# A graph layer's message loop in a written order, with PSUM banks shared by four groups and fewer, larger loads

## The chip, the cores and the metric

The kernel runs on one core of one Trainium2 chip. The core has five engines that run their own instruction queues: TensorE (PE; its weight loads are shown apart as PEld), VectorE (DVE), ScalarE (ACT), GpSimd (POOL) and SyncE (SP, which only issues transfers here). Results of TensorE go to PSUM, eight banks of 2 KB in each of 128 partitions; all else lives in SBUF or in device memory. The metric is device microseconds of one execution, the median of several.

## The reference

One layer of a graph network over 12,500 nodes (96 features) and 412,500 edges (4 features), the edges sorted by their target node. Cut to what matters:

```python
def mlp(h, W, b, gamma, beta):            # batch norm over all rows
    h = relu(h @ W + b)
    mu, var = mean(h, axis=0), mean(square(h - mean(h, axis=0)), axis=0)
    return gamma * (h - mu) * rsqrt(var + EPS) + beta

node_feat = mlp(x, W_node, b_node, g_node, beta_node)
edge_feat = mlp(edge_attr, W_edge, b_edge, g_edge, beta_edge)
message = concatenate([x[src], x[dst], edge_feat], axis=1)       # 412500 x 288
message = mlp(message, W_msg, b_msg, g_msg, beta_msg)
agg = segment_sum(message, dst, 12500)
out = layernorm(x + agg + node_feat)
```

## The kernel before, in words

All arithmetic is fp32. `x[src] @ W` and `x[dst] @ W` are not computed per edge: two tables in device memory, `p_tab` and `q_tab`, hold `x` times the two parts of `W_msg`. An edge's row of `p_tab` is fetched by an indirect transfer on GpSimd (L289), one instruction for 128 edges. `q_tab` needs no gather, since edges are sorted: 512 consecutive edges (a *group*, four tiles of 128) reach at most WN = 30 consecutive nodes, a window of `q_tab` that one matmul spreads over the edges.

There are 806 groups, and BG = 4 groups make a *block* (202 of them). The stages are:

1. **First table** (`table`, L136, called at L154): `p_tab`, in 7 chunks of 14 matmuls; PSUM tiles `pt` hold 4, 4, 4 and 2 of them, and DVE and ACT copy them out in turn. Then window offsets (`rel`, and `rel_d` in device memory, L191 to L200), by SP's loads `lin` and `first`.
2. **Second table** (`table` again, L310): `q_tab`, with four PSUM tiles `pt`. GpSimd already gathers the rows of the first 104 groups, 26 blocks (`blocks`, L297). Two staging buffers take a block each, 16 gathers, and SP writes each to device memory (`spill`, L303). The order of SP and GpSimd is written by hand here: the first spill stands behind the fourth chunk of `q_tab`, three more behind the seventh.
3. **Nodes** (L202): node features and their norm.
4. **Edge statistics** (`edge_norm`, L234): a first pass over the edge features. For each block of 2,048 edges, three matmuls of 512 columns into one PSUM tile of three banks (two such tiles), one ACT relu over the 1,536 columns (L252), three BN_STATS on DVE (L254). Features come in chunks of eight blocks (L245). Of 26 chunks, 19 have a spill behind them on SP.
5. **The message loop** (L326 to L430), over blocks in an order that mixes the 26 early blocks among the 176 late ones. For a late group GpSimd gathers into a ring of 30 buffers (`ring`, `ahead_of`, L294), 30 groups ahead. An early block's rows come back by one load (`fetch`, L401).
6. **End**: the final norm and layer norm (L598 to L631).

In the loop, per block: `load` (L342) fetches the block's edge features `ea`, one row of window offsets `rel_d`, and four windows of `q_tab` into `rhs`. `prepare` (L356) makes, by four matmuls into `pr` (four PSUM banks), the relu of the edge features (ACT, L364) and the 0/1 rows that select a node of the window (DVE, L365), both into `left`. Per group: `message` (L367) makes `z` by four matmuls of `left` with `rhs` (L371), writes the 0/1 columns of the target nodes into `h` (DVE, L373), adds the gathered rows (DVE, `hs`, L377; this frees the ring's buffer) and applies the relu (ACT, L378). `reduce` (L380) multiplies `h` with itself (L386, four matmuls accumulating into `pa`), which gives both the sums per node and the Gram matrix that the batch norm needs, and adds them to `agg` (L389) and `gram` (L390) on DVE. It runs one group behind `message`.

Edge features come from an array `eaq` in which each of the four groups of a block takes 32 partitions, of which 5 are used (4 features and a one) and the rest are zeros. In the loop a scheduler puts the instructions of each engine in order by itself; only the stages before it have a hand-written order, and that for SP and GpSimd alone. PSUM in the loop: four banks for `pr`, two for `z`, two for `pa`.

Of the kernel before, what the change touches and what calls it, by code (L numbers as in the profile page):

```python
# [50 lines left out]
WN = 30  # L51
# [3 lines left out]
RING = 30  # L55
J = 8
# [14 lines left out]
def gnn(ctx, tc, t):  # L71
# [64 lines left out]
    def table(out, w, work, ps, queues):  # L136

        rows = out.rearrange("(p b) f -> p b f", b=NB)
        for c in range(0, NB, CH):
            r = work.tile([P, CH, C], F32, name="trow", bufs=3)  # L140
            for j, i in enumerate(range(0, CH, NBK)):
                n = min(NBK, CH - i)
                pt = ps.tile([P, NBK, C], F32, name="pt", bufs=4)
                for g in range(n):
                    k = COL[c + i + g]
                    nc.tensor.matmul(pt[:, g, :], xp[:, k:k + P], w, start=True, stop=True)  # L146
                if j % 2:
                    nc.scalar.activation(r[:, i:i + n, :], pt[:, :n, :], AF.Copy)  # L148
                else:
                    nc.vector.tensor_copy(r[:, i:i + n, :], pt[:, :n, :])  # L150
            queues[c // CH % len(queues)].dma_start(rows[:, c:c + CH, :], r)
            yield

    with tc.tile_pool(name="win_w", bufs=1) as work, tc.tile_pool(name="win_ps", bufs=2, space=PSUM) as ps:  # L154
        for _ in table(p_tab, w_msg[:, 0, :], work, ps, (nc.sync, nc.scalar)):
            pass
# [77 lines left out]
    def edge_norm():  # L234

        with tc.tile_pool(name="es", bufs=2) as work, tc.tile_pool(name="es1", bufs=1) as one, \
                tc.tile_pool(name="es_ps", bufs=2, space=PSUM) as ps:
            stats = one.tile([P, NS, NBL, 6], F32, name="estats")
            for b in range(NBL):
# [7 lines left out]
                pr = ps.tile([P, NS, GE], F32, name="pr")  # L247
                for i in range(NS):
                    nc.tensor.matmul(pr[:, i, :], wide[Q * i:Q * i + 2 * EK, :],  # L249
                                     ea[Q * i:Q * i + 2 * EK, b % J, :], start=True, stop=True)  # L250
                r = work.tile([P, NS, GE], F32, name="r")
                nc.scalar.activation(r, pr, AF.Relu)  # L252
                for i in range(NS):
                    nc.vector.bn_stats(stats[:, i, b, :], r[:, i, :])  # L254
# [30 lines left out]
    def fast(ring):  # L285
# [22 lines left out]
        with tc.manual_schedule(engines={ET.SP, ET.Pool}):  # L308
            with tc.tile_pool(name="tab_w", bufs=1) as work, tc.tile_pool(name="tab_ps", bufs=2, space=PSUM) as ps:
                for i, _ in enumerate(table(q_tab, w_msg[:, 1, :], work, ps, (nc.sync,))):  # L310
                    if i in (3, 6):
                        next(store)
# [12 lines left out]

        with tc.tile_pool(name="fix", bufs=1) as fix, tc.tile_pool(name="msg", bufs=2) as work, \  # L326
# [3 lines left out]
            rhs = fix.tile([P, 2, BG, C], F32, name="rhs")  # L330
            nc.vector.tensor_copy(rhs[:C], w_e[:, None, None, :].to_broadcast([C, 2, BG, C]))
            for i in range(2):
                for k in range(BG):
                    nc.sync.dma_start(rhs[KR - 1:KR, i, k, :], bias)
# [3 lines left out]
            hb = [fix.tile([P, GT, P], F32, name=f"h{i}") for i in range(4)]  # L338
# [3 lines left out]
            def load(s, b):  # L342

                n = min(BG, NG - b * BG)
                ea = work.tile([P, GE], F32, name="ea")
                nc.sync.dma_start(ea, t["eaq"][:, b, :])
                nc.sync.dma_start(ea[EK:P:Q, :], rel_d[:, b * BG * GE:(b + 1) * BG * GE]
                                  .rearrange("o (g e) -> (o g) e", g=BG))
                _, val = nc.values_load_multi_w_load_instructions(
                    base[:, b * BG:(b + 1) * BG], engines=[ET.DVE, ET.SP], min_val=0, max_val=N - 1,  # L350
                    skip_runtime_bounds_check_because="they are nodes' numbers")
                for i in range(n):
                    nc.sync.dma_start(rhs[C:C + WN, s % 2, i, :], q_tab[bass.ds(val[i], WN), :])
                return ea, val

            def prepare(s, b, ea):  # L356

                n = min(BG, NG - b * BG)
                x = left[s % 2]
                pr = ps.tile([C + WN, BG, GE], F32, name="pr", bufs=1)  # L360
                for i in range(n):
                    nc.tensor.matmul(pr[:, i, :], we[Q * i:Q * i + EK + 1, :],  # L362
                                     ea[Q * i:Q * i + EK + 1, :], start=True, stop=True)
                nc.scalar.activation(x[:C, :n, :], pr[:C, :n, :], AF.Relu)  # L364
                nc.vector.tensor_scalar(x[C:C + WN, :n, :], pr[C:, :n, :], 0.0, None, op0=OP.is_equal)  # L365

            def message(s, g, h, pg):  # L367
                n = min(GT, NT - g * GT)
                z = ps.tile([P, GT, C], F32, name="z")
                for i in range(n):  # L370
                    nc.tensor.matmul(z[:, i, :], left[s % 2][:KR, g % BG, i * P:(i + 1) * P],  # L371
                                     rhs[:KR, s % 2, g % BG, :], start=True, stop=True)
# [7 lines left out]
            def reduce(g, h, val):  # L380

                n = min(GT, NT - g * GT)
                pa = ps.tile([C + 1, P], F32, name="pa")
# [4 lines left out]
                to = agg[:, bass.ds(val, WN)]  # L388
# [4 lines left out]
            early, late = list(range(SPILL // BG)), list(range(SPILL // BG, NBL))  # L393
            order = []
            for i, b in enumerate(late):
                order.append(b)
                while early and (SPILL // BG - len(early)) * len(late) < i * (SPILL // BG):
                    order.append(early.pop(0))
            order += early

            def fetch(b):  # L401
                if b * BG < SPILL:
                    back = work.tile([P, BG, GT, C], F32, name="pb")
                    nc.sync.dma_start(back, spill[b].rearrange("p g (a c) -> p g a c", a=GT))
                    for i in range(BG):
                        got[b * BG + i] = back[:, i, :, :]

            ea, val = load(0, order[0])
            prepare(0, order[0], ea)
            fetch(order[0])  # L410
            last, n, ahead = None, 0, SPILL + RING
            for s, b in enumerate(order):
                more = s + 1 < len(order)
                if more:
                    ea, then = load(s + 1, order[s + 1])
                    fetch(order[s + 1])
                for g in range(b * BG, min((b + 1) * BG, NG)):
                    if g % BG == 1 and more:
                        prepare(s + 1, order[s + 1], ea)
                    h = hb[n % len(hb)]  # L420
                    n += 1
                    message(s, g, h, got.pop(g))
                    if last:
                        reduce(*last)
                    last = g, h, val[g % BG]
                    if g >= SPILL and ahead < NG:
                        got[ahead] = ahead_of(ahead)
                        ahead += 1
                val = then
            reduce(*last)  # L430
# [237 lines left out]
```

## Time and profile before

| | us |
|---|---|
| time, median of 3 (4302.92 to 4304.81) | 4303.69 |
| the profiled execution's own time | 5713.74 |
| its span | 5712.0 |
| POOL busy, idle before its gathers | 3070.7, 1884.8 + 608.1 |
| PE busy | 3507.9 |
| DVE busy | 1830.5 |
| ACT busy | 1126.2 |

The profiled execution took 1410.05 us longer than the median, so its parts can't be read as parts of the median without asking which of them the recording lengthens. A busy time is that of instructions alone; transfers issued by an engine aren't counted as its work, save the indirect ones of GpSimd[...]. In the lists, "L289 POOL DMA_INDIRECT pg<-p_tab,src" is line, engine, operation, and what it writes from what; "issue" is waiting for which the profile shows no cause, and "remote" is a releaser that it can't name. In the timelines the columns are start, duration, then the instruction, and in brackets the engine's idle time before it with its releaser.

The core moved 315.48 MB in 190,423 packets. The largest issues, by the page:

```profile
ea<-in_eaq SPq DMA_DIRECT2D x202, 256.0 KB
pg<-p_tab,src POOLq DMA_INDIRECT x2807
spill<-stage SPq DMA_DIRECT2D x26, 768.0 KB
pb<-spill SPq DMA_DIRECT2D x26, 768.0 KB
rhs<-q_tab SPq DMA_DIRECT2D x806, 11.2 KB
```

### The profile page before, as it was taken

The page shows a single profiled execution, that of the slowest core. Times are in us where ns is not written, and L with a number is a line of the kernel's source. Part 1 is how long each engine was busy: PE and PEld are TensorE (multiplying, and loading weights), DVE is VectorE, ACT ScalarE, POOL GpSimd, SP SyncE. Part 2 cuts the span into 40 slices and gives each one's busy share as a digit, 9 for nine tenths or more (in the row PEclk, how much of TensorE's full clock was granted, in tenths as well). Part 3 has the DMA queues.
Part 4 walks back from the last instruction along what each step waited for, and adds up shares of the span by engine and source line. Part 5 has one row for each costly group of instructions (what it writes and reads, how often), then busy time and mean ns, then how long its engine had stood idle before and what let it go on. Part 6 is the DMA issues. An engine that isn't in the chain of part 4 may idle for free. (4 is left out here: it accounts for less than half of the span.)

```text
span 5712.0 us, 52958 instructions
## 1 busy us (share of the span) xinstructions
PE 3507.9 (61%) x16561; PEld 2613.4 (46%) x16561; DVE 1830.5 (32%) x4227; ACT 1126.2 (20%) x1304; POOL 3070.7 (54%) x3231
## 2 busy tenths in 40 slices
PE   3445666146666666766667566676566666665768
PEld 3331111024545455555555455455455555554547
DVE  1134555142323223232222232232322222322326
ACT  0113444021111111111111111111111111111113
POOL 2254444725555565555565555655555655556550
PEclk9955555557776666566666766666666666666667
DMA  3232323212222222222222222222222222222212
GB/s 117 73 97 56 70 63 68 47 42 51 52 52 49 46 50 52 50 52 49 52 46 51 50 51 49 47 52 49 51 50 52 46 50 52 49 52 46 50 44 82
DMA packets 190423, 315.48 MB, mean 55 GB/s; under 512 B 95817, under 2 KB 96201, under 8 KB 189128
## 3 DMA queue, kind: packets, MB, share of 16 engines
q0 software_dynamic: 103136, 158.62, 13.2%
q1 hardware_dynamic: 83502, 141.01, 8.9%
q10 hardware_dynamic: 3496, 12.36, 0.7%
q8 instruction: 137, 2.24, 0.2%
q14 instruction: 152, 1.25, 0.1%
HBM read 270.34 MB, written 41.37 MB: 55 GB/s over the span
## 5 line engine op out<-in xcount | busy, mean ns | idle before, releaser
L289 POOL DMA_INDIRECT pg<-p_tab,src x2807 | 2670.2, 951 | 1884.8 <-issue 787.5
L371 PE MATMUL z<-rhs,left 127*128 127x96 f32 x6446 | 1330.3, 350 | 706.3 <-issue 385.0
L371 PEld LDWEIGHTS z<-rhs,left 127*128 127x128 f32 x6446 | 1181.7, 261 | 1158.2 <-issue 684.0
L386 PE MATMUL pa<-h 128*97 128x127 f32 x6446 | 1236.4, 355 | 656.2 <-issue 351.7
L386 PEld LDWEIGHTS pa<-h 128*97 128x97 f32 x6446 | 1077.7, 230 | 719.8 <-issue 377.2
L378 ACT ACTIVATE h<-hs 128x384 f32<-128x384 f32 x806 | 419.5, 521 | 3094.3 <-DVE hs L377 1528.7
L389 DVE TENSOR_TENSOR agg<-pa,agg 97x30 f32 x806 | 150.4, 187 | 1978.1 <-PE z L371 752.6
L377 DVE TENSOR_TENSOR hs<-z,pg 128x384 f32<-128x384 f32 x702 | 390.2, 556 | 1054.7 <-issue 471.4
L289 POOL DMA_INDIRECT stage<-p_tab,src x416 | 399.6, 961 | 608.1 <-DMA spill<-stage 428.3
L362 PE MATMUL pr<-ea,we 6*126 6x512 f32 x1612 | 601.4, 841 | 157.4 <-issue 102.5
L249 PE MATMUL pr<-ea,wide 10*128 10x512 f32 x1212 | 406.6, 1107 | 409.2 <-ACT r L252 264.8
L254 DVE BATCH_NORM_STATS2 estats<-r 128x6 f32<-128x512 f32 x606 | 372.1, 680 | 442.6 <-ACT r L252 287.2
L364 ACT ACTIVATE left<-pr 96x2048 f32<-96x2048 f32 x202 | 376.3, 1863 | 549.9 <-remote 260.7
L365 DVE TENSOR_SCALAR left<-pr 30x2048 f32<-30x2048 f32 x202 | 462.9, 2292 | 43.8 <-ACT left L364 37.6
L249 PEld LDWEIGHTS pr<-ea,wide 10*128 10x128 f32 x1212 | 114.5, 307 | 700.0 <-ACT r L252 484.4
L252 ACT ACTIVATE r<-pr 128x1536 f32<-128x1536 f32 x202 | 292.2, 1451 | 592.9 <-remote 384.4
L362 PEld LDWEIGHTS pr<-ea,we 6*126 6x126 f32 x1612 | 150.6, 232 | 226.0 <-issue 150.3
L373 DVE TENSOR_TENSOR h<-rel,iota 128x120 f32<-128x120 f32 x806 | 204.9, 275 | 2.4 <-issue 0.4
L390 DVE TENSOR_TENSOR gram<-pa,gram 97x97 f32<-97x97 f32 x806 | 201.8, 250 | 0.3 <-DVE agg L389 0.3
L146 PE MATMUL pt<-w_msg,xp 96*128 96x96 f32 x392 | 85.6, 423 | 139.2 <-ACT trow L148 131.4
L146 PEld LDWEIGHTS pt<-w_msg,xp 96*128 96x128 f32 x392 | 84.1, 332 | 140.5 <-ACT trow L148 132.2
L223 PE MATMUL py<-center,xp 96*128 96x96 f32 x196 | 43.1, 423 | 60.5 <-DVE y0s L227 37.5
(95 smaller groups left out, 443.5 us busy)
## 6 DMA issues: line engine op xcount, KB each, us to landing
ea<-in_eaq SPq DMA_DIRECT2D x202, 256.0 KB
pg<-p_tab,src POOLq DMA_INDIRECT x2807
spill<-stage SPq DMA_DIRECT2D x26, 768.0 KB
pb<-spill SPq DMA_DIRECT2D x26, 768.0 KB
rhs<-q_tab SPq DMA_DIRECT2D x806, 11.2 KB
ea<-in_ea SPq DMA_DIRECT2D x75, 160.0 KB
stage<-p_tab,src POOLq DMA_INDIRECT x416
q_tab<-trow SPq DMA_DIRECT2D x7, 672.0 KB
```

Of the source, the lines that this page charges most:

```text
L249: nc.tensor.matmul(pr[:, i, :], wide[Q * i:Q * i + 2 * EK, :], ea[Q * i:Q * i + 2 * EK, b % J, :], start=True, stop=True)
L252: nc.scalar.activation(r, pr, AF.Relu)
L254: nc.vector.bn_stats(stats[:, i, b, :], r[:, i, :])
L289: nc.gpsimd.indirect_dma_start(out=pg[:, i, :], out_offset=None, in_=p_tab[:, :], in_offset=bass.IndirectOffsetOnAxis(ap=src[:, k:k + 1], ...
L362: nc.tensor.matmul(pr[:, i, :], we[Q * i:Q * i + EK + 1, :], ea[Q * i:Q * i + EK + 1, :], start=True, stop=True)
L364: nc.scalar.activation(x[:C, :n, :], pr[:C, :n, :], AF.Relu)
L365: nc.vector.tensor_scalar(x[C:C + WN, :n, :], pr[C:, :n, :], 0.0, None, op0=OP.is_equal)
L371: nc.tensor.matmul(z[:, i, :], left[s % 2][:KR, g % BG, i * P:(i + 1) * P], rhs[:KR, s % 2, g % BG, :], start=True, stop=True)
L373: nc.vector.tensor_tensor(h[:, :, C + 1:C + 1 + WN], rel[:, g, :].unsqueeze(2).to_broadcast([P, GT, WN]), iota[:, None, :].to_broadcast([P ...
L377: nc.vector.tensor_add(hs[:, :n, :], z[:, :n, :], pg[:, :n, :])
L378: nc.scalar.activation(h[:, :n, :C], hs[:, :n, :], AF.Relu)
L386: nc.tensor.matmul(pa[:, :C + 1 + WN], h[:r, i, :C + 1], h[:r, i, :C + 1 + WN], start=i == 0, stop=i == n - 1)
```

## The change

What it does:

- The window is 31 nodes for 30, which makes the contraction of `z` 128 rows and the columns of `pa` 128.
- The second table has eight PSUM tiles for four (the first keeps four).
- Edge statistics: the matmuls are taken in pairs over block borders, two banks to a PSUM tile, four tiles; one ACT relu over 1,024 columns and two BN_STATS for each pair, and four buffers for the relu's result instead of two.
- The loop's instructions are in the written order on all five engines. In the turn of group k: `z` of group k + 1, the message of k, the sums of k - 1, the next block's edge matmuls (first group of a block), half of `prepare` (third and fourth group each), the additions of group k - 5 to `agg` and `gram`, the gather of a later group.
- The sums of four groups lie in one PSUM bank, in two such tiles; six buffers `h` for four; `rhs` has three slots for two and is loaded two blocks ahead, and so are the edge features.
- Edge features come from the compact array `ea`, two blocks at a time, in four transfers of 5 partitions with 4 KB each, and `rel_d` for both blocks in one; `eaq` is gone.
- DVE reads the block's window numbers where it first needs them, SP reads its own in `load`.

The core of the diff:

```diff
-WN = 30
+WN = 31
+SKEW = 5
+HB, RB = 6, 3
+CL, CE = 2, 2
...
-                pt = ps.tile([P, NBK, C], F32, name="pt", bufs=4)
+                pt = ps.tile([P, NBK, C], F32, name="pt", bufs=bufs)
...
-                for i, _ in enumerate(table(q_tab, w_msg[:, 1, :], work, ps, (nc.sync,))):
+                for i, _ in enumerate(table(q_tab, w_msg[:, 1, :], work, ps, (nc.sync,), 8)):
...
-                pr = ps.tile([P, NS, GE], F32, name="pr")
                 for i in range(NS):
-                    nc.tensor.matmul(pr[:, i, :], wide[Q * i:Q * i + 2 * EK, :],
+                    k = NS * b + i
+                    if k % 2 == 0:
+                        pr = ps.tile([P, 2, GE], F32, name="pr")
+                    nc.tensor.matmul(pr[:, k % 2, :], wide[Q * i:Q * i + 2 * EK, :],
                                      ea[Q * i:Q * i + 2 * EK, b % J, :], start=True, stop=True)
-                r = work.tile([P, NS, GE], F32, name="r")
-                nc.scalar.activation(r, pr, AF.Relu)
-                for i in range(NS):
-                    nc.vector.bn_stats(stats[:, i, b, :], r[:, i, :])
+                    if k % 2:
+                        r = work.tile([P, 2, GE], F32, name="r", bufs=4)
+                        nc.scalar.activation(r, pr, AF.Relu)
+                        for o in (1, 0):
+                            nc.vector.bn_stats(stats[:, (k - o) % NS, (k - o) // NS, :], r[:, 1 - o, :])
...
-                ea = work.tile([P, GE], F32, name="ea")
-                nc.sync.dma_start(ea, t["eaq"][:, b, :])
-                nc.sync.dma_start(ea[EK:P:Q, :], rel_d[:, b * BG * GE:(b + 1) * BG * GE]
-                                  .rearrange("o (g e) -> (o g) e", g=BG))
+                if c not in eas:
+                    o = min(o, NBL - c)
+                    eas[c] = work.tile([P, o, GE], F32, name="ea" if b >= first else "eae")
+                    for i in range(BG):
+                        nc.sync.dma_start(eas[c][Q * i:Q * i + EK, :, :], t["ea"][EK * i:EK * (i + 1), c:c + o, :])
+                    nc.sync.dma_start(eas[c][EK:P:Q, :, :], rel_d[:, c * BG * GE:(c + o) * BG * GE]
+                                      .rearrange("o (b g e) -> (o g) b e", g=BG, e=GE))
...
-                nc.scalar.activation(x[:C, :n, :], pr[:C, :n, :], AF.Relu)
-                nc.vector.tensor_scalar(x[C:C + WN, :n, :], pr[C:, :n, :], 0.0, None, op0=OP.is_equal)
+                part = slice(i, min(i + BG // 2, NG - order[s] * BG))
+                if part.start < part.stop:
+                    pr, x = prs[s], left[s % 2]
+                    nc.scalar.activation(x[:C, part, :], pr[:C, part, :], AF.Relu)
+                    nc.vector.tensor_scalar(x[C:C + WN, part, :], pr[C:, part, :], 0.0, None, op0=OP.is_equal)
...
-                pa = ps.tile([C + 1, P], F32, name="pa")
+                if k % 4 == 0:
+                    pas[k // 4] = ps.tile([C + 1, 4, P], F32, name="pa")
+                pa = pas[k // 4][:, k % 4, :]
...
+            with tc.manual_schedule(engines={ET.SP, ET.Pool, ET.PE, ET.DVE, ET.Activation}):
+                load(0)
+                fetch(0)
+                load(1)
+                edges(0)
+                prepare(0, 0)
+                prepare(0, BG // 2)
+                linear(0)
+                for k in range(n + SKEW):
+                    s, g = steps[min(k, n - 1)]
+                    if k < n and g % BG == 0:
+                        if s + 2 < len(order):
+                            load(s + 2)
+                        if s + 1 < len(order):
+                            fetch(s + 1)
+                    if k + 1 < n:
+                        linear(k + 1)
+                    if k < n:
+                        message(k)
+                    if 0 <= k - 1 < n:
+                        sums(k - 1)
+                    if k < n and s + 1 < len(order):
+                        if g % BG == 0:
+                            edges(s + 1)
+                        if g % BG >= BG // 2:
+                            prepare(s + 1, (g % BG - BG // 2) * (BG // 2))
+                    if k >= SKEW:
+                        add(k - SKEW)
+                    if k < n and g >= SPILL and ahead < NG:
+                        got[ahead] = ahead_of(ahead)
+                        ahead += 1
```

`linear` holds the four matmuls of `z`, `message` the 0/1 columns, the addition of the gathered rows and the relu, `sums` the four matmuls into `pa`, `add` the two additions to `agg` and `gram`, `edges` the four matmuls into `pr`; their instructions are those of before.

## The prediction, made before the changed kernel was run

> **What bounds the kernel now.** I read the page's first two parts first, then the groups of GpSimd (POOL) and its waits, then three short timelines. The timed median is 4303.69 us; the profiled execution took 5713.74 us, of which 5712.0 is the span and 1.7 lies around it. A third more is too much to pass over: the profile must first be made to agree with the clock.
>
> ```profile
> span 5712.0 us, 52958 instructions
> PE 3507.9 (61%) x16561; PEld 2613.4 (46%) x16561; DVE 1830.5 (32%) x4227; ACT 1126.2 (20%) x1304; POOL 3070.7 (54%) x3231
> ...
> L289 POOL DMA_INDIRECT pg<-p_tab,src x2807 | 2670.2, 951 | 1884.8 <-issue 787.5
> ...
> L289 POOL DMA_INDIRECT stage<-p_tab,src x416 | 399.6, 961 | 608.1 <-DMA spill<-stage 428.3
> ```
>
> Most of the 3231 POOL instructions are the 2807 + 416 = 3223 gathers. Each is 0.95 us busy, and successive ones start 1.25 us apart, 0.30 us of it "issue". Next, POOL's waits, and its restart after the longest:
>
> ```profile
> POOL pg L289 <- issue: 787.5, 2499, 2.7
> POOL pg L289 <- DVE h L373: 584.2, 83, 15.6
> POOL stage L289 <- DMA spill<-stage: 428.3, 13, 137.7
> POOL pg L289 <- DVE gram L390: 300.6, 94, 6.4
> POOL pg L289 <- DVE hs L377: 174.8, 30, 87.3
> ```
>
> ```profile
> 236.21 0.95 POOL L289 DMA_INDIRECT stage<-p_tab,src  x1 [137.68 <-DMA spill<-stage]
> ```
>
> In the profile POOL waits 1060 us for DVE to free ring buffers, so the consumers look like the bound. But see what they do there, and what they do once the last gather is out:
>
> ```profile
> 3012.30 0.95 POOL L289 DMA_INDIRECT pg<-p_tab,src  x1 [0.30 <-issue]
> 3014.17 0.32 PE L371 MATMUL z<-rhs,left 127*128 127x96 f32 x1 [0.39 <-issue]
> ...
> 3016.31 0.19 DVE L389 TENSOR_TENSOR agg<-pa,agg 97x30 f32 x1 [12.45 <-remote]
> ...
> 5563.29 0.94 POOL L289 DMA_INDIRECT pg<-p_tab,src  x1 [0.30 <-issue]
> ```
>
> ```profile
> 5611.94 2.30 DVE L365 TENSOR_SCALAR left<-pr 30x2048 f32<-30x2048 f32 x1
> ...
> 5621.61 2.30 DVE L365 TENSOR_SCALAR left<-pr 30x2048 f32<-30x2048 f32 x1
> ...
> 5648.48 0.25 DVE L390 TENSOR_TENSOR gram<-pa,gram 97x97 f32<-97x97 f32 x1
> ```
>
> While gathers run, DVE and PE repeatedly stand still for up to 12 us ("remote", "issue") without any program dependency shown; POOL goes on at 1.25 us. After 5563 the stalls are gone: one block of four groups takes 5621.61 - 5611.94 = 9.67 us, 2.42 us per group. I take the stalls to be mostly the recording's, because the clock says so. Add up POOL alone: first gather at 55.3; the 137.7 us wait for the first spill; 3069.8 busy + 3223 x 0.30 = 4036.7; after the last gather about 2.0 to land (priced below) and five groups x 2.42 = 12.1; from the last L390 to the end of the span 5712.0 - 5648.5 = 63.5; 1.7 around. Sum 4309.0 against the median 4303.69, 0.12% away. Without the recording POOL is busy almost throughout; in the loop it asks (2807 - 120) x 1.25 / 806 = 4.17 us per group where the other engines need 2.42.
>
> **What the Trainium skill says.** "Perfetto Trace Analysis", section on the SWDGE DMA instruction: the profiled end of a GpSimd DMA is when the last DSP has written its descriptors, not when data have moved. So 0.95 us is POOL's own work; the trace agrees, since it hardly varies (951 and 961 ns). "DMA: Bandwidth & Descriptors", anatomy of one DMA: some 2.0 us fixed from issue to completion, the estimate used above for the last gather; no row shows it. "TensorE: Matmul & The Clock Gate", part 1: the clock is halved while PE is little used; here the page grants 0.5 in the edge-statistics stage and 1.0 in 5606 to 5640. "PSUM — Partial Sum Buffer", bank collisions: two engines may not touch one bank at once; hence sums of four groups in one bank may be read only when all four are written, which the lag of five groups allows.
>
> **The change part by part.**
> Gathers: order, count and waits (a ring buffer freed by DVE, the gather eight before) stay. Nothing is taken from 4036.7.
>
> Second table, 8 PSUM tiles for 4: the part on POOL's path. POOL waits at 98 to 236 us for the first spill, which stands on SP behind four chunks of q_tab:
>
> ```profile
> 211.28 1.02 DVE L150 COPY trow<-pt 128x384 f32<-128x384 f32 x2 [18.31 <-DMA rel_d<-rlin]
> ...
> 211.96 36.15 PE L146 MATMUL pt<-w_msg,xp 96*128 96x96 f32 x168 [130.93 <-ACT trow L148]
> ...
> 231.21 0.33 SPq L303 DMA_DIRECT2D spill<-stage  x1
> ```
>
> PE had one chunk (14 matmuls) done when the copies resume at 211.3, then needs 36.15/84 = 0.43 us per matmul: three chunks, to 230. After, eight tiles hold two chunks, as PE's order shows (28 matmuls before the first wait); two remain, and the spill leaves 14 x 0.43 = 6.0 us sooner. The copies (four, 2.0 us per chunk) are no limit. POOL and the node stage behind it all move 6.0 us forward. The next spills could eat this: their stages last 16 x 1.25 = 20.0 us and SP reaches them 18 us later in both kernels, so I keep it: -6.0 (bounds 0 and -8).
>
> Edge statistics, tiles of two matmuls, four deep. Same 606 BN_STATS, which set the pace:
>
> ```profile
> 702.02 22.18 DVE L254 BATCH_NORM_STATS2 estats<-r 128x6 f32<-128x512 f32 x36 [0.25 <-ACT r L252]
> ...
> 5638.61 1.02 ACT L364 ACTIVATE left<-pr 96x1024 f32<-96x1024 f32 x1 [0.75 <-PE pr L362]
> ```
>
> 0.616 us each, 24 per chunk of eight blocks: 14.8 us. ACT goes from 202 of 1451 ns to 303 of about 1.02 us; with the 0.26 us it waited for PE, 12 x 1.28 = 15.4 per chunk, with the longer 0.59 us, 19.3. POOL's 19 stages beside 25.25 chunks take 380 us, 15.05 per chunk, and the second stage buffer lends 20 us: it waits only above (380 + 20)/25.25 = 15.84. I take 15.4, cost 0; with the cover gone, up to (19.3 - 15.84) x 25.25 = 87.
>
> Loop: written order, halves of prepare (1.02 x 2 for 1.86 on ACT, 1.23 x 2 for 2.30 on DVE, 0.3 us per block), 128 columns for 127, window 31 for 30. PE already is busy 33.48 of 34 us in 5606 to 5640, so I see 2.3 to 2.5 per group. All lie beneath POOL's 4.17; cover gone, 0.1 x 806 = 81 us either way.
>
> SP: per pair of blocks 2 x 128 packets of 2 KB become 20 of 4 KB, 404 issues become 505, rhs is loaded two blocks ahead past fetch and rel_d. DMA engines are some 20% busy and "pg <- DMA" waits total 29.9 us in steps of 0.3: cost between 0 and -10, taken 0. TensorLoads are divided between SP and DVE, same count.
>
> Ends: four bias DMAs more (5.03 us for eight) beside a ring that still holds 120 x 1.25 = 150 us of gathers: 0. Four more sums are added after the last matmul: 4 x (0.19 + 0.25) = +1.8, perhaps 1 back in the last five groups: +1.
>
> Sum: 4303.7 - 6.0 + 1.0 = 4298.7; 4299. Against the profiled 5713.74 I forecast no equal step: fewer packets and a fixed order will shorten the recorded stalls, and the profiled time may fall by hundreds.
>
> **Rivals.**
> Main, POOL's chain: 4285 to 4312. For it: the sum of 4309. Against: unproved that recording causes the stalls. Chance 0.57.
> Faster: the stalls are partly real, and timed gathers quicker than 1.25. For it: they come only while gathers run. Against: the sum leaves them no room. If 160 us of 4303 (a tenth of the 2492.9 - 966.9 = 1526 us that POOL idles in the profile beyond its issue gaps) go: 4140; range 4050 to 4280. Chance 0.19.
> Slower: ACT in the edge statistics takes the place of DVE. Pairs at 1.6 us instead of 1.28 make 19.3 per chunk, above 15.84; spills come late, POOL waits; the last chunks have no stage beside them, so I take some 50 of the 87: 4299 + 50 = 4349. It decides from 1.32 us per pair, little above what I take; against it, four tiles deep let PE run ahead. Chance 0.20.
> Not doing what it says: the early matmuls of the second table do not start early; then 4305, inside main's range. Another 0.04 for something slower unseen.
>
> **How the numbers follow.** A difference of 0.2%, 8.6 us, is what a measurement of this kernel can tell. Main splits into 0.13 faster, 0.41 same, 0.03 slower; the faster rival adds 0.18 and 0.01; the slower ones 0.24. Faster 0.31, same 0.42, slower 0.27. Main's own range is 4285 to 4312; signs being mixed, the 8-in-10 range reaches to 4200 (half the faster rival) and 4350.
>
> **What would show it.** Right: gathers again 3223 x 1.25; first spill near 225 and POOL's longest wait near 132 us; POOL waiting for DVE less in the profile, with little of that in the time. Wrong: a time under 4280 (POOL was not the bound), edge statistics above 16 us per chunk with new "spill" waits, or PE in the loop at half clock and above 4.17 us per group.

## The result and the profile after

| | us | ratio to before (95%) |
|---|---|---|
| before, median of 5 (4300.59 to 4304.81) | 4302.92 | |
| after, median of 5 (4319.23 to 4323.89) | 4321.2 | 1.0045 (1.0034 to 1.0056) |
| after, profiled execution, its span | 4319.5 | |

The change makes the kernel 18.3 us slower. The forecast was 4299, no change; 4321.2 lies inside its range of 4200 to 4350, but on the wrong side of before, and the one slower rival that it named (ACT in the edge statistics) is not what happened: what came is the 0.04 that it kept for something slower unseen.

The same kernel takes quite another time from one occasion to the next, the kernel before 4301 to 4304 us on some (the "first kind" below) and 5661.6 to 5726.85 on others (the "second kind"), so that the profile of before (5712.0) and its median (4303.69) are of different kinds, and ratios are only taken within one.

The profile after is of the first kind, though it was recorded like that of before. From its page, the span, the busy times and four groups (busy, mean ns of one, then idle time before it and what ended most of it):

```profile
span 4319.5 us, 52615 instructions
PE 2829.6 (66%) x16561; PEld 2359.9 (55%) x16561; DVE 1853.1 (43%) x4430; ACT 1141.4 (26%) x1606; POOL 3071.2 (71%) x3231
...
L295 POOL DMA_INDIRECT pg<-p_tab,src x2807 | 2671.5, 952 | 855.4 <-issue 657.6
...
L295 POOL DMA_INDIRECT stage<-p_tab,src x416 | 398.8, 959 | 324.0 <-DMA spill<-stage 133.9
...
L260 DVE BATCH_NORM_STATS2 estats<-r 128x6 f32<-128x512 f32 x606 | 361.9, 676 | 46.0 <-ACT r L258 46.0
L258 ACT ACTIVATE r<-pr 128x1024 f32<-128x1024 f32 x303 | 295.0, 1024 | 158.2 <-PE pr L254 129.0
```

POOL's waits in the whole run (us in total, times, longest):

```profile
POOL pg L295 <- issue: 657.6, 2158, 0.3
POOL pg L295 <- DMA pg<-p_tab,src: 137.5, 451, 0.3
POOL stage L295 <- DMA spill<-stage: 133.9, 4, 131.0
...
POOL stage L295 <- DMA stage<-p_tab,src: 15.0, 17, 1.9
```

No wait of POOL in the loop is longer than 0.3 us, the pause between any two gathers: the loop is bound by POOL's instructions alone, and DVE never holds back a ring buffer. The prediction's sum holds here in its large parts. The second table does what it was said to do; SP's and POOL's timelines around the first spill:

```profile
223.23 0.33 SPq L309 DMA_DIRECT2D spill<-stage  x1
```

```profile
228.66 0.94 POOL L295 DMA_INDIRECT stage<-p_tab,src  x1 [130.95 <-DMA spill<-stage]
```

223.2 was forecast near 225, 131 near 132. So POOL gained at the start and still ended later. Two of the rows above show where to look: "stage <- DMA stage", 15.0 us in 17 waits of up to 1.9, and the mean gather of 952 ns. In the timeline's rows after 800 us, where the loop runs alone, a gather of after takes 0.9497 us on average (2745 of them); 0.94 is the commonest value, and 160 of them take over 1.0. These rows are rounded to 0.01 us, which puts all means of this kind below some 0.002 us under the exact ones (0.9518 here); only their differences are used.

### The profile page after: what moved, and what is told of

The parts are those of the page before. It is cut to its first block, busy times and chain, and to the rows that moved or that the text cites. A ratio compares the mean times of both kernels' runs of the same rounds, so it can differ in the third digit from the quotient of the medians.

```text
span 4319.5 us, 52615 instructions
## 1 busy us (share of the span) xinstructions
PE 2829.6 (66%) x16561; PEld 2359.9 (55%) x16561; DVE 1853.1 (43%) x4430; ACT 1141.4 (26%) x1606; POOL 3071.2 (71%) x3231
## 3 DMA queue, kind: packets, MB, share of 16 engines
q14 instruction: 152, 1.25, 0.1%
## 5 line engine op out<-in xcount | busy, mean ns | idle before, releaser
L295 POOL DMA_INDIRECT pg<-p_tab,src x2807 | 2671.5, 952 | 855.4 <-issue 657.6
L409 PE MATMUL z<-rhs,left 128*128 128x96 f32 x6446 | 1146.3, 336 | 1222.6 <-issue 849.5
L409 PEld LDWEIGHTS z<-rhs,left 128*128 128x128 f32 x6446 | 1039.2, 245 | 1463.5 <-issue 922.8
L433 PE MATMUL pa<-h 128*97 128x128 f32 x6446 | 1077.1, 322 | 5.4 <-ACT h L421 5.4
L433 PEld LDWEIGHTS pa<-h 128*97 128x97 f32 x6446 | 959.1, 206 | 5.9 <-ACT h L421 5.9
L402 DVE TENSOR_SCALAR left<-pr 31x1024 f32<-31x1024 f32 x403 | 495.4, 1229 | 641.1 <-ACT left L401 641.1
L401 ACT ACTIVATE left<-pr 96x1024 f32<-96x1024 f32 x403 | 403.8, 1002 | 17.1 <-DMA rhs<-q_tab 15.9
L258 ACT ACTIVATE r<-pr 128x1024 f32<-128x1024 f32 x303 | 295.0, 1024 | 158.2 <-PE pr L254 129.0
L416 DVE TENSOR_TENSOR h<-rel,iota 128x124 f32<-128x124 f32 x806 | 223.1, 277 | 0.2
L393 PE MATMUL pr<-ea,we 6*127 6x512 f32 x1404 | 202.4, 645 | 21.8 <-DMA ea<-rel_d 12.2
L445 DVE TENSOR_TENSOR agg<-pa,agg 97x31 f32 x806 | 150.7, 187 | 28.0 <-PE pa L433 3.9
## 6 DMA issues: line engine op xcount, KB each, us to landing
rhs<-q_tab SPq DMA_DIRECT2D x806, 11.6 KB
```

The lines of the kernel that those rows point to most:

```text
L295: nc.gpsimd.indirect_dma_start(out=pg[:, i, :], out_offset=None, in_=p_tab[:, :], in_offset=bass.IndirectOffsetOnAxis(ap=src[:, k:k + 1], ...
L393: nc.tensor.matmul(prs[s][:, i, :], we[Q * i:Q * i + EK + 1, :], block[s][Q * i:Q * i + EK + 1, :], start=True, stop=True)
L401: nc.scalar.activation(x[:C, part, :], pr[:C, part, :], AF.Relu)
L402: nc.vector.tensor_scalar(x[C:C + WN, part, :], pr[C:, part, :], 0.0, None, op0=OP.is_equal)
L409: nc.tensor.matmul(zs[k][:, i, :], left[s % 2][:KR, g % BG, i * P:(i + 1) * P], rhs[:KR, s % RB, g % BG, :], start=True, stop=True)
L416: nc.vector.tensor_tensor(h[:, :, C + 1:C + 1 + WN], rel[:, g, :].unsqueeze(2).to_broadcast([P, GT, WN]), iota[:, None, :].to_broadcast([P ...
```

## The experiments

### Which half of the change: a cross, and the second table alone

Two kernels cross the halves: the new loop behind the old second table and edge statistics, and the old loop behind the new ones. A third has only the eight PSUM tiles, a fourth is the changed kernel with WN = 30.

a_oldhead, against the changed kernel (the rest of the edge statistics goes back with it):

```diff
-                for i, _ in enumerate(table(q_tab, w_msg[:, 1, :], work, ps, (nc.sync,), 8)):
+                for i, _ in enumerate(table(q_tab, w_msg[:, 1, :], work, ps, (nc.sync,), 4)):
...
-                    if k % 2 == 0:
-                        pr = ps.tile([P, 2, GE], F32, name="pr")
+                pr = ps.tile([P, NS, GE], F32, name="pr")
...
```

b_newhead is the kernel before with both of these the other way round, b_q8 the kernel before with the 8 alone. a_wn30, against the changed kernel:

```diff
-WN = 31
+WN = 30
```

> The changed loop behind the old second table (four PSUM tiles) and the old edge statistics (three banks to a tile). Theory 'head' (the pairs of edge statistics crowd the DMA engines and the spills, and POOL pays some 14 us of new waits between 300 and 700 us): 4303 to 4311, that is the time before or the 6 us of the second table more, and a loop whose gathers follow at the same pace as in the changed kernel. Theory 'loop' (the written order, the wider window or the small transfers make the timed loop some 18 to 24 us longer): 4321 to 4328, POOL's first wait back at 137 us.

> The other half of the cross: the old loop behind the new second table and the new edge statistics. Theory 'head': 4311 to 4322, as slow as the changed kernel. Theory 'loop': 4297, the 6 us of the second table less than before. If both halves show nothing and only the two together do, the head and the loop interact, and each of the crossed kernels stands within 6 us of 4303.

> The kernel before with eight PSUM tiles in the second table and nothing else. The prediction's first step says 4303 - 6 = 4297, with the first spill issued near 225 us and POOL's longest wait near 132 us; if what POOL gains there is lost again at a later spill, 4303 with a longer wait at the second or third stage.

> The changed kernel with a window of 30 nodes for 31: contraction 127, windows of 11.2 KB, 30 rows and 120 columns on DVE. Theory 'head': 4321, no change. Theory 'loop' by the window (POOL's instruction lengthened beside DVE's and the transfers' work): a few us less, 4310 to 4318; if the window is none of it, 4321.

Measured, all of the first kind (before 4303.13 beside them):

| | us | ratio (95%) | mean gather after 800 us | POOL's waits for landed rows of the stages |
|---|---|---|---|---|
| b_q8 | 4298.25 | 0.9987 (0.9981 to 0.9994) | 0.9427 | 3.2 |
| b_newhead | 4308.63 | 1.0014 (1.0008 to 1.0021) | 0.9431 | 17.2 |
| a_oldhead | 4333.87 | 1.007 (1.0056 to 1.0084) | 0.9530 | 14.6 |
| a_wn30 | 4333.42 | 1.007 (1.0056 to 1.0084) | 0.9516 | 20.0 |

- The second table's tiles bring 4.9 us by the medians (5.6 by the ratio, 0.0013 x 4303; 6.0 forecast). POOL's longest wait is 138.2 us with four tiles (a_oldhead) and 131 to 133.5 with eight.
- The new edge statistics cost 4308.63 - 4298.25 = 10.4 us on the old loop. That is the first part of the loss; b_newhead lies between its two theories (4297 and 4311 or more).
- The new loop costs more than that, and the cost is in the gathers' own duration: 0.943 us with the old loop, 0.950 to 0.953 with the new. Over 2745 gathers, 0.0067 x 2745 = 18 us for after, 28 for a_oldhead. The expectation of "loop" for a_oldhead (at most 4328) was still too low, and a_wn30 was expected to stay or gain and lost 12 us: the size of this cost is not fixed by the loop, it shifts with things that only move the loop in time.

b_q8 also gives what the profile of before does not, a trace of the old loop of the first kind. Its gathers, from the page:

```profile
L289 POOL DMA_INDIRECT pg<-p_tab,src x2807 | 2652.7, 945 | 855.5 <-issue 777.2
L289 POOL DMA_INDIRECT stage<-p_tab,src x416 | 397.0, 954 | 319.1 <-DMA spill<-stage 136.3
```

The same count, the same idle time (855.5 against 855.4); 2671.5 - 2652.7 = 18.8 us more busy in after. This part of the loss hides in "busy", where no view of waits shows it.

### What lengthens a gather

Look at one long gather of after, in POOL's and DVE's timeline:

```profile
1620.63 0.56 DVE L420 TENSOR_TENSOR hs<-z,pg 128x384 f32<-128x384 f32 x1 [4.07 <-DMA pg<-p_tab,src]
...
1621.72 0.25 DVE L446 TENSOR_TENSOR gram<-pa,gram 97x97 f32<-97x97 f32 x1
1621.78 1.21 POOL L295 DMA_INDIRECT pg<-p_tab,src  x1 [0.31 <-DMA pg<-p_tab,src]
1621.89 0.28 DVE L416 TENSOR_TENSOR h<-rel,iota 128x124 f32<-128x124 f32 x1
1623.29 0.94 POOL L295 DMA_INDIRECT pg<-p_tab,src  x1 [0.30 <-issue]
```

L416 writes the 0/1 columns; it starts 0.11 us into the gather and ends at 1622.17; the gather ends at 1622.99, 0.82 later. An undisturbed one takes 0.94, so this one stood still from about 0.94 - 0.82 = 0.12 us after its start until L416 was done. I call a gather "met" when L416 runs at any time from 0.10 to 0.17 us after its start, and count in 1500 to 2500 us of each trace:

```
kernel      gathers  met by L416  their mean  all others' mean  over 1.0 us (met by L416)
after           796           78       1.031            0.9417                 46 (all 46)
a_oldhead       795           79       1.051            0.9414                 52 (all 52)
a_wn30          795           74       1.058            0.9415                 56 (all 56)
b_q8            801           25       0.987            0.9411                  5 (all 5)
b_newhead       801           18       1.006            0.9417                  4 (all 4)
```

In after all 46 long gathers end 0.80 to 0.83 us after the end of the columns that met them. The 295 gathers that met another operation of DVE at that moment (hs 153, left 119, agg 16, gram 7) have means of 0.940 to 0.942. The whole loop agrees: in no trace of the first kind does a gather that isn't met take over 0.97 us, and above the 0.944 us of those the met ones add up to 21.9 us in after, 27.8 in a_wn30, 30.9 in a_oldhead, but 4.1 in b_q8 and 4.2 in b_newhead.

So it is this one operation: it takes both its inputs (`rel`, `iota`) from SBUF, while the others have one in PSUM. The Trainium skill has the mechanism, in "SBUF — State Buffer", section "SBUF: two separate sides": GpSimd shares a pair of SBUF ports with DVE, a DVE operation with two SBUF inputs locks it against a GpSimd instruction that reads SBUF, and the loser waits until the lock is given back. The traces agree that one waits for the other, and in both directions: in a_hfirst6 (below) 13 columns that start within some 0.03 us of a gather's start take 0.30 to 0.35 us for 0.28, and their gathers the usual 0.94. They differ from the page in one point. There the first to come keeps the ports for its whole instruction; here only a moment of the gather is exposed, near its start (presumably when it reads its indices), and 138 columns of after that start 0.15 to 0.60 us into a gather take their 0.28 us and delay nothing. That the two SBUF inputs are the reason is the page's account; no run here changed them.

Why the written order meets that moment more often: hs starts when a group's rows have landed, which keeps nearly a fixed distance to the gathers (0.10 us after one's start above), and the next gather starts 1.25 us behind the last. In after, agg and gram stand between hs and the next columns, in half of the groups `left` too: the columns then start 0.73 to 0.90 us behind hs, more where agg has to wait (1.26 above), or 3.64 past `left`. In the order of before half of the columns (397 of 794 in b_q8) stand right behind hs, 0.47 us behind its start, in the middle of a gather. The test moves this one instruction:

```diff
+            def columns(k):
+                nc.vector.tensor_tensor(
+                    hb[k % HB][:, :, C + 1:C + 1 + WN],
+                    rel[:, steps[k][1], :].unsqueeze(2).to_broadcast([P, GT, WN]),
+                    iota[:, None, :].to_broadcast([P, GT, WN]), op=OP.is_equal)
...
-                nc.vector.tensor_tensor(
-                    h[:, :, C + 1:C + 1 + WN], rel[:, g, :].unsqueeze(2).to_broadcast([P, GT, WN]),
-                    iota[:, None, :].to_broadcast([P, GT, WN]), op=OP.is_equal)
...
+                columns(0)
...
                         message(k)
+                        if k + 1 < n:
+                            columns(k + 1)
```

> The changed kernel with one DVE instruction moved: the 0/1 columns of group k + 1 are written right behind the addition hs of group k, so that they run some 0.6 us behind the landing of a group's rows instead of 1.0 to 1.1. Theory 'collision' (an SBUF-to-SBUF operation of DVE that runs in the first 0.3 us of a gather's instruction holds that instruction up): the mean gather of the loop falls from 0.9497 to some 0.943 us, 2745 x 0.0067 = 18 us, and the time to 4303 +- 4. Theory 'transfers' (the smaller, denser loads of SP lengthen the gathers): 4321, gathers still 0.950.

It met five occasions of the second kind (below) before one of the first, a_hfirst6:

> The changed kernel with the 0/1 columns of group k + 1 written right behind hs of group k. Where the kernel before takes 4303 us: 'collision' says a mean gather of 0.943 us in the loop for 0.9497 and 4303 +- 4; 'transfers' says 4321 and 0.950. Where it takes 5660 or more: 0.974 to 0.980 of it again.

Measured: 4303.89 us (4302.27 to 4306.2), before 4301.25 beside it, ratio 1.0006 (0.9998 to 1.0015). The loop's mean gather is 0.9424, 24 of 2749 over 1.0; in the window of the table 31 are met, mean 0.965. The page and DVE's and POOL's timelines:

```profile
L295 POOL DMA_INDIRECT pg<-p_tab,src x2807 | 2651.6, 945 | 855.6 <-issue 659.6
```

```profile
1620.03 0.56 DVE L423 TENSOR_TENSOR hs<-z,pg 128x384 f32<-128x384 f32 x1 [4.01 <-DMA pg<-p_tab,src]
1620.51 0.28 DVE L413 TENSOR_TENSOR h<-rel,iota 128x124 f32<-128x124 f32 x1
```

```profile
1619.92 0.94 POOL L295 DMA_INDIRECT pg<-p_tab,src  x1 [0.30 <-issue]
1621.17 0.94 POOL L295 DMA_INDIRECT pg<-p_tab,src  x1 [0.30 <-DMA pg<-p_tab,src]
```

The columns end at 1620.79, before the gather of 1621.17 starts. POOL's busy time in these gathers falls by 2671.5 - 2651.6 = 19.9 us and the time by 17.3 (4321.2 to 4303.9; by the ratios, 0.0039 x 4303 = 16.8). "Transfers" falls: all of SP's new loads are still there.

But the place in time is only a part of what the move changed. After 800 us, columns that start up to 0.17 us before a gather became rarer (199 in after, 57 in a_hfirst6). Those that start in a gather's first 0.11 us became more (38 and 54), yet all 38 made a gather of over 1.0 us, and of the 54 only one did. One of the others, with columns that meet the gather as defined above:

```profile
1870.56 0.56 DVE L423 TENSOR_TENSOR hs<-z,pg 128x384 f32<-128x384 f32 x1 [0.78 <-DMA pg<-p_tab,src]
1870.95 0.94 POOL L295 DMA_INDIRECT pg<-p_tab,src  x1 [0.30 <-issue]
1871.04 0.28 DVE L413 TENSOR_TENSOR h<-rel,iota 128x124 f32<-128x124 f32 x1
```

What differs is DVE's operation right before the columns: gram in after, hs here. The other traces say the same: behind gram 273 of 275 such starts made a long gather (a_oldhead, a_wn30 and the first columns of a_htwice2, below), behind hs 3 of 106 (a_hfirst6 and a_best3). The rarer early columns are worth some 11 us of the gathers' time (14.2 to 2.9), the other neighbour some 7 (7.5 to 0.1). Why the neighbour matters is not shown.

The opposite test writes the columns twice at their old place:

```diff
                 nc.vector.tensor_tensor(
                     h[:, :, C + 1:C + 1 + WN], rel[:, g, :].unsqueeze(2).to_broadcast([P, GT, WN]),
                     iota[:, None, :].to_broadcast([P, GT, WN]), op=OP.is_equal)
+                nc.vector.tensor_tensor(
+                    h[:, :, C + 1:C + 1 + WN], rel[:, g, :].unsqueeze(2).to_broadcast([P, GT, WN]),
+                    iota[:, None, :].to_broadcast([P, GT, WN]), op=OP.is_equal)
```

> The changed kernel with the 0/1 columns written twice in a row at their old place, same values. Where the kernel before takes 4303 us: 'collision' says a mean gather above 0.953 us in the loop for 0.9497 and 4328 to 4343; 'DVE is hidden beneath POOL whatever it does' says 4321.

Measured: 4335.7 us (4333.15 to 4336.78), ratio 1.0073 (1.006 to 1.0087), mean gather 0.9529 in the loop, 161 of 794 met. The time is as "collision" said, the mean gather 0.0001 short of it. In part that is luck: of the 14.5 us (4335.7 - 4321.2; 12.0 by the ratios) the gathers of the loop show 2680.0 - 2671.5 = 8.5, and some 6 are longer waits of POOL before the loop (133.5 us for 131.0 at the first spill, 18.5 for 15.0 for landed rows), where no columns are written. DVE is 43% busy in after and no wait of POOL for it is longer than the pause, and still 0.28 us more of it per group costs those 8.5 us. The second columns of a pair, which start some 0.03 us after the first have ended, never held up a gather that they started in (0 of 109 in its first 0.11 us).

### What the edge statistics cost

In b_newhead and after, POOL waits for rows of its own: in the staging buffers a gather may start only when the one eight before has landed. These waits in b_q8 and in b_newhead:

```profile
POOL stage L289 <- DMA stage<-p_tab,src: 3.2, 3, 1.7
POOL stage L292 <- DMA stage<-p_tab,src: 17.2, 16, 2.3
```

SP's and POOL's timelines of after, then SP's of b_q8:

```profile
457.44 0.35 SPq L309 DMA_DIRECT2D spill<-stage  x1
457.95 7.70 SPq L248 DMA_DIRECT2D ea<-in_ea  x6
```

```profile
468.89 0.94 POOL L295 DMA_INDIRECT stage<-p_tab,src  x1 [0.59 <-DMA stage<-p_tab,src]
471.25 0.95 POOL L295 DMA_INDIRECT stage<-p_tab,src  x1 [1.41 <-issue]
...
476.77 0.94 POOL L295 DMA_INDIRECT stage<-p_tab,src  x1 [0.84 <-DMA stage<-p_tab,src]
```

```profile
459.30 0.35 SPq L303 DMA_DIRECT2D spill<-stage  x1
461.99 17.52 SPq L245 DMA_DIRECT2D ea<-in_ea  x6
```

In after the edge features (480 KB for a chunk, here two) follow the spill (768 KB) after 0.51 us, and the gathers that are issued meanwhile land late: the waits come 11 to 19 us behind. In b_q8 the loads come 2.7 us later and drag on for 17.5 us, because their buffers are not yet free, and no gather waits. This is regular. In eight traces of the first kind I took each spill from 360 us to the end of the edge statistics and the next load behind it, and counted a gather as late where POOL waits over 0.5 us for it before the next spill:

```
load behind its spill by    spills    of them with a late gather    these waits beyond the pause, us in all
under 1 us                      74                            61                       75.7
1 us or more                    76                             0                        0.0
```

So the waits come with loads that start right behind a spill, that is, when SP stands waiting at a spill while the next chunk's buffer is already free. The new statistics have time to spare: from 400 to 700 us PE is busy 282.3 of 300 us in b_newhead and 285.7 in after, but 300.0 in b_q8. That the two transfers side by side are what delays the gathers is argued from the table and not shown by an experiment. Whether the loads' place on SP's queue can be changed to advantage was tried with ACT's queue (b_nh_act, against b_newhead):

```diff
-                        nc.sync.dma_start(ea[Q * i:Q * i + 2 * EK, :n, :],
+                        nc.scalar.dma_start(ea[Q * i:Q * i + 2 * EK, :n, :],
```

> The kernel before with the new second table and the new edge statistics, whose features ACT's queue loads instead of SP's. Where the kernel before takes 4303 us: if a load right behind a spill is what delays the gathers, the waits of POOL for landed rows fall from 17.2 to under 8 us and the time from 4308.6 to 4299 to 4304; if the higher rate of the loads does it, 4308 stays.

Measured: 4477.53 us (4476.93 to 4478.66), ratio 1.0405 (1.0391 to 1.0419), far off. From 400 to 800 us POOL waits for nothing over 0.3 us, as was expected, but the edge statistics themselves now get their features only every 20 us (ACT's relu waits 220.4 us for spills, which its loads now stand behind) and run until 1013 us instead of 749; the ring fills and POOL waits 178.9 us for the first hs. The statistics being thinned out, the experiment can't tell place from rate. It failed as a test.

The remaining one, a_best, is a_hfirst with the old edge statistics (as in a_oldhead's diff, its second part alone):

> The changed kernel with the columns moved and the old edge statistics, eight PSUM tiles in the second table kept. Where the kernel before takes 4303 us: 4304 - 10 = 4294 (4291 to 4298), because the pairs' waits for landed rows go; POOL's waits for landed rows of the staging buffers fall from 15 to 3 to 8 us. If the pairs are not the reason, 4304.

Measured: 4300.12 us (4298.29 to 4304.63), ratio 0.9994 (0.9986 to 1.0002): above the 4294 expected. The waits for landed rows are still 13.4 us (18.1 in a_hfirst6; 3 to 8 were expected): also with the old statistics a load stands under 1 us behind its spill in 8 of 19 cases here, against 2 of 19 in b_q8. So it is not the pairs as such: they cost 10.4 us on the old loop and 3.8 us here (4303.89 - 4300.12, the ratios' intervals overlap). Why the same statistics keep a larger distance in b_q8 than in a_best stays open. The lowest median is that of b_q8, the kernel before with eight tiles: 4298.25, with an interval that overlaps a_best's.

### The second kind of occasion

The kernels of the last sections first met this kind, in the same form and with expectations meant for the first:

> The changed kernel with the 0/1 columns written twice in a row, same values, 806 x 0.28 us more of DVE, which idles over half of the loop. Theory 'collision': the pair covers 0.56 us instead of 0.28, more gathers meet it: excess of the loop's gathers grows from some 13 us to 20 to 35 us, the time to 4328 to 4343. Theory 'DVE is hidden beneath POOL, whatever it does': 4321.

> The changed kernel with the columns moved as in the run before and the old edge statistics (three banks to a tile, two tiles), with the second table's eight PSUM tiles kept. Theories 'collision' and 'head' together: 4303 - 10 = 4293 to 4298, as fast as the kernel before with eight tiles alone (4298.25) or a little faster. If the loop of the change has another cost that is hidden in the timing, it stays above 4303.

> The kernel before with the new second table and the new edge statistics, whose edge features are loaded by ACT's queue instead of SP's, so that a load no longer stands behind a spill in one queue. Theory: SP's order puts every load 0.5 us behind a spill, both fill the DMA engines at once, gathers land more than eight gathers late, 10.4 us lost against eight tiles alone. Then the waits of POOL for landed rows of the staging buffers fall from 17.2 to under 8 us and the time from 4308.6 to 4299 to 4304. If the pairs themselves are what delays the gathers (the higher rate of the loads, not their place), 4308 stays.

Then a_hfirst and a_best again, and at last the changed kernel itself beside them:

> The changed kernel with the 0/1 columns of group k + 1 written right behind hs of group k, once more, since in the run before this one the kernel before itself took 5661.6 us (as in its profile) and PE, not POOL, set the loop's pace. Where the kernel before takes 4303: theory 'collision': the mean gather of the loop falls from 0.9497 to some 0.943 us, the time to 4303 +- 4. Theory 'transfers' (SP's smaller, denser loads lengthen the gathers): 4321, gathers still 0.950.

> The same move with the old edge statistics, once more for the same reason. Where the kernel before takes 4303: 'collision' and 'head' together give 4293 to 4298, as fast as the kernel before with eight tiles alone (4298.25) or a little faster; above 4303 if the changed loop has another cost.

> A third time: the changed kernel with the 0/1 columns of group k + 1 written right behind hs of group k. Where the kernel before takes 4303 us: 'collision' says a mean gather of 0.943 us in the loop for 0.9497 and 4303 +- 4; 'transfers' says 4321 and 0.950. Where the kernel before takes 5660 or more, PE's pace sets the loop and some 5520 to 5610 come again.

> The changed kernel with the 0/1 columns of group k + 1 written right behind hs of group k, on another occasion. Where the kernel before takes 4303 us: 'collision' says a mean gather of 0.943 us in the loop for 0.9497 and 4303 +- 4; 'transfers' says 4321 and 0.950.

> Columns of group k + 1 right behind hs of group k. Where the kernel before takes 4303 us: 'collision' says 4303 +- 4 and a mean gather of 0.943 us in the loop, 'transfers' 4321 and 0.950. Where it takes 5660 or more: 0.974 to 0.980 of it, as in the runs so far.

> The changed kernel itself on the same chip. Where the kernel before takes 4303: 4321. Where it takes 5660 or more, PE's pace sets the loop: if the moved columns matter only for POOL's gathers, within 0.3% of the kernel with the columns moved, that is 2.0 to 2.7% faster than before; if the move brings something to DVE's chain there, slower than it by more.

| | us | before beside it | ratio (95%) |
|---|---|---|---|
| after_again | 5589.63 | 5716.78 | 0.9772 (0.9759 to 0.9785) |
| a_hfirst5 | 5598.13 | 5716.78 | 0.9791 (0.9778 to 0.9804) |
| a_hfirst, a_hfirst4 | 5523.85, 5518.81 | 5661.6, 5669.24 | 0.976, 0.9737 (0.9721 to 0.9773 over both) |
| a_hfirst2, a_hfirst3 | 5612.19, 5603.02 | 5726.85, 5718.28 | 0.9799, 0.98 (0.9786 to 0.9813) |
| a_htwice | 5576.46 | 5661.6 | 0.9851 (0.9835 to 0.9866) |
| a_best, a_best2 | 5553.11, 5646.68 | 5661.6, 5726.85 | 0.9816, 0.9859 (0.9802 to 0.9874 over both) |
| b_nh_act | 5759.93 | 5661.6 | 1.0174 (1.0161 to 1.0188) |

The expectations for 4303 us can't be judged here; those of a_hfirst3, a_hfirst5, a_hfirst6 and after_again were made for both kinds, and a_hfirst3, a_hfirst5 and after_again came out as they said for this one. Here the change is 2.3% faster, and moving the columns brings nothing (5598.13 against 5589.63). POOL does not set the pace, as in the profile of before; after_again's group of gathers and three of PE's groups of matmuls:

```profile
L295 POOL DMA_INDIRECT pg<-p_tab,src x2807 | 2680.4, 955 | 1798.3 <-issue 744.1
```

```profile
3002.03 1.10 PE L433 MATMUL pa<-h 128*97 128x128 f32 x3 [1.08 <-issue]
...
3004.85 1.10 PE L433 MATMUL pa<-h 128*97 128x128 f32 x3 [1.73 <-issue]
...
3007.68 0.58 PE L433 MATMUL pa<-h 128*97 128x128 f32 x2 [1.73 <-issue]
```

Pauses of 1.08 and 1.73 us without a releaser stand between matmuls that otherwise follow one another without any, and POOL idles 1798.3 us before its gathers instead of 855. What makes PE pause there is not shown. The recording alone doesn't, since the profiled executions of the first kind were recorded too (4319.5 us for after), nor does the chip alone: six chips are on record, and one of them (11) with both kinds. What sets the kind stays open.

## Why the prediction was wrong, point by point

- **The bound** was right for the clock: POOL's chain of 3223 gathers. **Its reason** was wrong: the stalls in the profile of before were taken to be the recording's. They belong to the occasion. The sum came near the median by errors that cancel, which is luck: the gathers' busy time was 3069.8, where b_q8 shows 2652.7 + 397.0 = 3049.7; their pause averages 0.305 us in the loop, not 0.30 (0.005 x 3223 = 16 us more); and from the last gather's start to the end of the span are 69 us (4319.5 - 4250.35), where the sum had 2.0 + 12.1 + 63.5 = 77.6.
- **Second table**: right, 4.9 us for 6.0.
- **Gathers** ("Nothing is taken from 4036.7") and **Loop** ("All lie beneath POOL's 4.17") are the steps that failed. They asked whether DVE's work fits into POOL's time, and it does. They did not ask whether DVE can hold up POOL's instruction while it runs. The term priced at 0 measured 16.8 to 19.9 us. "It hardly varies (951 and 961 ns)" compared two means, and missed the spread within one of them. The rows to notice stood in the profile of before, some nine microseconds ahead of the first that the prediction shows of its loop:

```profile
3003.39 0.47 DVE L373 TENSOR_TENSOR h<-rel,iota 128x120 f32<-128x120 f32 x2
3003.48 1.01 POOL L289 DMA_INDIRECT pg<-p_tab,src  x1 [0.30 <-issue]
```

  A gather of 1.01 us among neighbours of 0.95, beside the columns.
- **Edge statistics**: the pace was right (BN_STATS waited only 46.0 us for ACT, and the slower rival did not occur); the cost of 0 was wrong by 10.4 us on the old loop. The term compared chunks with POOL's pace and stopped there. Statistics that are a little faster than POOL are not harmless: SP then sends a load right behind most spills (11 of 19 in after), and with these come the late gathers.
- **SP's fewer packets** and **ends**: 0 and +1, and nothing was seen of either: a_hfirst6 has all of the loop's changes and stands at 1.0006, b_newhead with the old loop at 1.0014, and their intervals overlap.
- **The profiled time** was to fall by hundreds. It did, from 5713.74 to 4321.2, but because the occasion was another; where both were of the second kind, the time fell by 127 us (5716.78 to 5589.63).
- **The clock**: "halved while PE is little used" does not fit the stage that it is tied to. From 400 to 700 us PE is busy 300.0 of 300 us in b_q8, and the granted clock is 0.50. Nothing in the sum rests on it.

The account, by ratios times 4303: -5.6 (tiles), +11.6 (edge statistics), -3.4 (the loop's rest, within the error), +16.8 (columns) = +19.4, the measured 0.0045. Each term is the step from one measured kernel to the next, so the sum agrees by construction; that each step is one cause is what the sections above argue.

## What to carry to other kernels

Where GpSimd's gathers are the bound, its instruction's own duration is a cost to watch: compare its mean and its spread before and after, and try other places for DVE operations with two SBUF inputs: here the place behind gram cost, the place behind hs hardly did. An engine that is mostly idle can still cost time by when it runs. And before a profile is read as parts of a measured time, find out whether the two were taken under the same conditions, by timing the kernel again beside the profile.

## What was not expected of the hardware

- A gather is held up only near its start, by a DVE operation with two SBUF inputs, and by as much as is left of that operation: up to 1.21 us for 0.94 in after. Behind gram such an operation still holds it up when it starts 0.11 us into the gather (38 of 38 in after), behind hs it doesn't (1 of 54 in a_hfirst6).
- The size of this depends on the phase: with the same loop 22 to 31 us in all (after 21.9, a_wn30 27.8, a_oldhead 30.9), when only the head or the window differs.
- The same kernel takes 4303 or 5660 to 5727 us from one occasion to the next, and the change has another sign on each: 1.0045 and 0.9772.
